# Moving the early steps of a block to its third, fifth and seventh step, doing part of a first step inside a statistics chain, and one scheduling region to the end

## The chip, the cores and the metric

The kernel runs on one core of one Trainium2 chip. The metric is the device time in microseconds of that core, the median of three runs. A profiled execution gives, beside its time, a trace of every instruction on the engines: TensorE (PE, with its weight loads as PEld), VectorE (DVE), ScalarE (ACT), GpSimd (POOL) and SyncE (SP), which here only issues DMAs.

## The reference

The input x is 1 x 384 x 192 x 192 in 32-bit floats. Two residual layers follow each other, each on a group-normalized input (32 groups of 12 channels, over all pixels):

```python
x = x + _L0_conv_ref(_gn(x), ...)
x = x + _L1_conv_ref(_gn(x), ...)
```

The first layer multiplies by a 1152 x 384 matrix (q, k and v), takes the maximum of each 2 x 2 square of pixels, and runs a 3 x 3 depthwise convolution. Of q and k only the norms of their rows and the Gram matrix of 8 heads of 48 channels are needed; four softmaxes, each over the largest 24, 32, 36 or 38 entries of a row, are summed with weights of 0.2 and multiplied by v; a GELU, a doubling of rows and columns, and a 384 x 384 projection give what is added to x. The second layer adds seven depthwise convolutions (13 x 13, and six smaller ones, some dilated), each with its own batch normalization; the kernel merges them into one 13 x 13 filter per channel.

## The kernel before

Channels lie on the 128 partitions, in three chunks (NJ = 3, called j). The kernel goes through four stages.

Statistics. All of x is read once in blocks, chunk after chunk, and each block's mean and variance are taken. When a chunk is complete, its groups' mean and variance are made by `group_stats`, a generator: small matmuls average over the channels of a group, others spread the mean again, VectorE forms the variance's summand, matmuls average that, ScalarE takes the root, VectorE inverts, and last matmuls spread the coefficients to the channels (gn0). Each `yield` is a place where the caller can put other instructions. Since a group is complete with its chunks, the product of the q and k weights with the first pixels can begin early, chunk by chunk: for 18 pairs (B, m) in EARLY (blocks B = 0 to 5, tiles m = 0 to 2 of the q rows, first half of the block) the products with chunks 0 and 1 are made during the statistics (`first_chunk`, `early`, `multiply`, line 420) and put by in the unused space of v (`put_by`, line 431). The last two of these wait for the chain of the third chunk (LATE = 2), and that chain, with nothing to read any more, stands alone at the end of this stage.

First pass. 24 blocks of 8 rows of x; each block has 12 steps, one for each of six tiles m of q and k (m = 0 to 2 is q, 3 to 5 is k) and each half sb of the block. `turns` gives the order of the tiles. A step multiplies (`project`, line 654: six matmuls in the program, each of which the trace shows as two), takes the 2 x 2 maximum on VectorE (`pool`, line 666), adds the bias on ScalarE (line 673), and, after both halves of a tile, `taps` (line 702) adds the eight outer taps of the 3 x 3 filter on VectorE, four in each of two later steps. The products go to one of two PSUM buffers (`qkvps`), so a step can start when the maximum of the step two before it has been read. For a step in EARLY, `fill` (line 260) first copies what was put by back into the PSUM buffer, on ScalarE, and only chunk 2 is multiplied: a short step. When a block's last tile is ready, `turn` (line 731) transposes q and k, and `add_gram` (line 743) adds their product to the Gram matrix; both are done in the fourth to seventh step of the next block. `normalize` (line 634) and GpSimd's `sum_up` (lines 271 to 273) prepare the next block in the seventh step and after.

Second pass and projection. v is made in the same way, the softmaxes run meanwhile, and then 72 projection steps (three chunks of 24 blocks; lines 1418 to 1439) make the first layer's output. In each, ScalarE evicts and stores it (line 1426), and VectorE adds it to loaded sums of x and takes statistics (lines 1434 and 1435). The statistics of the second layer's input are made by `derive`, a generator that calls `group_stats` and that `advance` moves on by one `yield` a projection step. The first two chunks' `derive` run inside the projection; the third one's starts behind it and is moved on once in each block of the convolution.

Convolution. 48 blocks of 8 channels. `arrange` (line 1338) transposes a block's input on VectorE, `patch` (line 1305) corrects its taps, `convolve` (line 1356) makes 8 groups of ten matmuls (as the trace shows them) into one of four PSUM buffers, ScalarE evicts each group into co (line 1364), and `finish` stores it.

The order of instructions on each engine is written out by hand inside a `manual_schedule` region; outside of it, and where one region ends and the next begins, a planner places them. The projection and the convolution were two such regions, with the closing and opening of memory pools between them. Memory that one pool frees is used by the next: the first writer waits for the last reader.

Of the kernel before, what the change touches and what calls it, by code (L numbers as in the profile page):

```python
# [7 lines left out]
F32 = mybir.dt.float32  # L8
# [6 lines left out]
P = 128  # L15
# [24 lines left out]
CC = 8  # L40
# [17 lines left out]
def tile_attn_then_large_kernel_conv(ctx: ExitStack, tc: tile.TileContext, a: dict, out: bass.AP):  # L58
# [42 lines left out]
    def group_stats(pool, psum, mv, name, gw, terms, outs, apart=False):  # L101
# [17 lines left out]
        yield  # L119

# [161 lines left out]
    with (  # L282
# [173 lines left out]
        def early():  # L456
# [5 lines left out]
            for n, (B, m) in enumerate(EARLY):  # L462
# [8 lines left out]
                if n == len(EARLY) - 1:  # L471
                    yield True
# [86 lines left out]
        for _ in range(5):  # L559
            next(last)  # L560
        next(first)
        pc = in_one(last)
        nc.vector.tensor_copy(gn0[:, 2:], pc[:, 2:])
        normalize(0, 0, 2)
        next(first)
        fill(0, 0, 0)
        normalize(0, 1, 2)
        next(first)
# [8 lines left out]
    ctx_l1 = ExitStack()  # L577
    with ctx_v:
# [396 lines left out]
        turns = [m + s * NJ for m in range(NJ) for s in range(2)] + [2 * NJ + m for m in range(NJ)]  # L975
# [427 lines left out]
        with (  # L1403
# [4 lines left out]
            with tc.manual_schedule():  # L1408
                for n in range(NJ * NBB):
                    i, b = divmod(n, NBB)  # L1410
                    if n + 4 < NJ * NBB:
                        load_sum(n + 4)
                    if b == 0 and i > 0:
                        running.append(derive(i - 1, stats1))
                    advance()
                    ps = b2_ps.tile([P, NBK], F32, tag="pj", name="pj")
                    for j in range(NJ):
                        nc.tensor.matmul(  # L1418
                            ps,
                            lhsT=wp[:, j, i * P : (i + 1) * P],  # L1420
                            rhs=v[:, j, b * RB : (b + 1) * RB, :].rearrange("p r w -> p (r w)"),
                            start=(j == 0),
                            stop=(j == NJ - 1),
                        )
                    pj = by.tile([P, 2, RB // 2, WS], F32, tag="pjs", name="pjs", bufs=6)
                    nc.scalar.activation(  # L1426
                        pj.rearrange("p y r w -> p r y w"),
                        ps.rearrange("p (r y w) -> p r y w", y=2, w=WS),
                        AF.Identity,
                        bias=bpj[:, i : i + 1],  # L1430
                    )
                    t = by.tile([P, NBK], F32, tag="cell", name="cell", bufs=1)
                    sm = smj.pop(n)
                    nc.vector.scalar_tensor_tensor(t, sm, quarter[:, i : i + 1], ps, ALU.mult, ALU.add)
                    nc.vector.bn_stats(stats1[:, i, b, :], t)
                    if i == 0:
                        nc.vector.bn_stats(stats_s[:, i, b, :], sm)
                    pd = pds[i]
                    nc.scalar.dma_start(
                        out=bass.AP(  # L1440
                            pd.tensor,
                            pd.offset + b * NBK // 2,
                            [[HS // 2 * WS, P], [P * HS // 2 * WS, 2], [1, NBK // 2]],
                        ),
                        in_=pj.rearrange("p y r w -> p y (r w)"),
                    )
                    if n == NBB + 8:
                        running.append(load_rows(0, nc.gpsimd))
                    if n == NBB:
                        running.append(load_taps(0, nc.gpsimd, 1))  # L1450
                    if n == NBB + 14:
                        running.append(residual(0, nc.vector, 3))
                    if n == NBB + 20:
                        assert not running
                        patch(0)
                        for q in range(3):
                            normalize1(0, q)
                        first = arrange(0, 1)
                    if n > NBB + 20 and n % 3 < 2:
                        next(first, None)  # L1460

                    if n == NBB + 22:
                        running.append(load_rows(1, nc.gpsimd))
                    if n == 2 * NBB + 8:
                        second = residual(1, nc.vector, 3)
                    if n >= 2 * NBB + 8 and (n % 3 == 2 or n > 2 * NBB + 16):
                        next(second, None)
                    if n == 3 * NBB - 4:
                        assert next(first, first) is first and next(second, second) is second
                    if n >= 3 * NBB - 4 and n < 3 * NBB - 1:  # L1470
                        normalize1(1, n - (3 * NBB - 4))
                while running:
                    advance()
                running.append(derive(NJ - 1, stats1))
                advance()

    with (
        tc.tile_pool(name="l2", bufs=1) as l2,  # L1480
        tc.tile_pool(name="more", bufs=1) as more,
        tc.tile_pool(name="lo", bufs=2) as lo,
# [83 lines left out]
```

## Time and profile before

| | us |
|---|---|
| median of 3 runs | 3060.59 |
| lowest and highest | 3058.51, 3060.72 |
| the profiled execution | 3060.02 |
| its span, first to last instruction | 3058.1 |
| TensorE busy | 2932.1 (96%) |
| VectorE busy | 2518.0 (82%) |
| ScalarE busy | 1348.5 (44%) |
| GpSimd busy | 935.2 (31%) |

In the profile a line gives the start, the length, the engine, the line of the kernel, the operation, what it writes from what it reads with shapes, and how many instructions are merged in it. In brackets stands how long the engine was idle before it and what ended the wait. A table by stretch gives, for each engine, the busy time and the number of instructions, then the clock that TensorE was granted as a share of the full one, the DMA share and the bandwidth.

### The profile page before, as it was taken

Reading aid. Unit: us, or ns where it says so; the run is one execution under the profiler, and the core shown is the slowest. Engines: PE = TensorE matmul, PEld = TensorE weight load, DVE = VectorE, ACT = ScalarE, POOL = GpSimd, SP = SyncE. Lnnn points to the kernel's source line nnn. Section 1 sums busy time; section 2 is a strip of 40 time slices with the busy share of each in tenths; the row PEclk is TensorE's granted clock in tenths of the full one; section 3 lists DMA queues with packets and bytes.
Section 4 is the critical chain, followed back from the end, with each engine's and each line's share of the span. In section 5 each row is a group of like instructions: output and inputs, shape, how many; then the busy total and the mean of one; then the engine's idle time right before and its main releaser. Section 6 shows DMA issues by size and latency. Waiting matters only on the chain.

```text
span 3058.1 us, 32274 instructions
## 1 busy us (share of the span) xinstructions
PE 2932.1 (96%) x10860; PEld 1944.7 (64%) x10860; DVE 2518.0 (82%) x3507; ACT 1348.5 (44%) x2465; POOL 935.2 (31%) x1150
## 2 busy tenths in 40 slices
PE   0799999999999999999999999999999999999998
PEld 0355666666666666665555555555777777777776
DVE  6879888787878787879998989888788777777775
ACT  3745554454444444444444444732333333333332
POOL 4242124242423232312222222501333333333332
PEclk9899999999999999999999999999999999999999
DMA  9934243342424242423333332677999999999984
GB/s 392 415 118 146 94 142 126 106 138 97 145 86 153 82 158 77 154 93 101 101 108 125 104 101 70 198 222 203 274 253 243 246 243 243 247 246 243 247 219 116
DMA packets 275926, 525.76 MB, mean 172 GB/s; under 512 B 25954, under 2 KB 190480, under 8 KB 275632
## 3 DMA queue, kind: packets, MB, share of 16 engines
q1 hardware_dynamic: 204432, 326.44, 37.6%
q0 software_dynamic: 49376, 174.29, 18.0%
q10 hardware_dynamic: 21952, 22.95, 2.2%
q8 instruction: 87, 1.43, 0.2%
q14 instruction: 79, 0.65, 0.1%
HBM read 362.23 MB, written 161.37 MB: 171 GB/s over the span
## 4 chain that ended last, share of the span: by engine, by line
PE 85%; DVE 9%; DMA 3%; issue 1%; ACT 1%; POOL 0%; ACTq 0%; POOLq 0%; DVEq 0%
PE qkv L654 46%; PE conv L1356 29%; PE pj L1418 4%; DVE v L702 3%; DMA xs<-in_x 2%; PE av L1110 2%; DVE mx L666 2%; PE gram L743 2%; DVE acc L702 2%; PE tr L731 2%; PE qkv L420 1%; DVE stats L526 1%; DMA smj<-sums 0%; DMA v<-in_x 0%; DVE xp L1338 0%
## 5 line engine op out<-in xcount | busy, mean ns | idle before, releaser
L654 PE MATMUL qkv<-xt,wqk 128*128 128x384 f32 x3312 | 1087.3, 487 | 5.5 <-ACT qkv L260 3.4
L1356 PE MATMUL conv<-xp,wt 128*128 128x288 f32 (+1 forms) x3840 | 917.7, 402 | 2.2 <-ACT co L1364 2.2
L654 PEld LDWEIGHTS qkv<-xt,wqk 128*128 128x128 f32 x3312 | 620.7, 190 | 424.7 <-DVE mx L666 8.0
L1356 PEld LDWEIGHTS conv<-xp,wt 128*128 128x128 f32 x3840 | 729.0, 190 | 188.5 <-ACT co L1364 2.6
L702 DVE SCALAR_TENSOR_TENSOR acc<-pooled,wd,acc 128x384 f32<-128x384 f32 (+2 forms) x1152 | 734.1, 637 | 30.5
L673 ACT ACTIVATE pooled<-mx,bq 128x192 f32<-128x192 f32 x432 | 196.8, 456 | 903.6 <-DVE mx L666 902.2
L1338 DVE STREAM_TRANSPOSE xp<-xn 128x4608 f32<-128x4608 f32 (+1 forms) x107 | 442.0, 4131 | 172.5 <-PE conv L1356 163.4
L666 DVE TENSOR_REDUCE mx<-qkv 128x192 f32<-128x768 f32 x432 | 412.1, 954 | 203.4 <-PE qkv L654 187.5
L654 PE MATMUL qkv<-xt,wv 128*128 128x384 f32 x1728 | 562.4, 487 | 2.5 <-DVE mx L666 2.2
L654 PEld LDWEIGHTS qkv<-xt,wv 128*128 128x128 f32 x1728 | 326.1, 190 | 233.4 <-DVE mx L666 9.8
L1364 ACT ACTIVATE co<-conv,cb 128x288 f32<-128x288 f32 x384 | 191.5, 500 | 600.6 <-PE conv L1356 590.3
L702 DVE SCALAR_TENSOR_TENSOR v<-pooled,wd,v 128x384 f32<-128x384 f32 (+2 forms) x576 | 376.3, 653 | 15.2
L271 POOL TENSOR_TENSOR sum<-xt 128x192 f32<-128x192 f32 x128 | 87.4, 683 | 955.0 <-ACT xt L634 943.1
L1381 POOL DMA_DIRECT2D out<-o x191 | 105.9, 584 | 571.3 <-DVE o L1372 513.6
L634 ACT ACTIVATE xt<-xt,gn 128x768 f32<-128x768 f32 x278 | 275.5, 1014 | 0.0
L1315 POOL TENSOR_TENSOR raw<-raw,up 128x2496 f32<-128x2496 f32 x46 | 230.8, 5017 | 22.5 <-DMA up<-pd 21.3
L1372 DVE STREAM_TRANSPOSE o<-co 128x2304 f32<-128x2304 f32 (+1 forms) x50 | 209.8, 4199 | 19.8 <-ACT co L1364 19.8
L1418 PE MATMUL pj<-v,wp 128*128 128x384 f32 x432 | 144.9, 495 | 0.9 <-ACT gx L1121 0.6
L771 POOL DMA_DIRECT2D zd<-v x96 | 72.0, 757 | 218.9 <-ACT v L762 218.2
L1418 PEld LDWEIGHTS pj<-v,wp 128*128 128x128 f32 x432 | 82.3, 193 | 56.7 <-issue 2.1
L272 POOL TENSOR_TENSOR sum<-sum,xt 128x192 f32<-128x192 f32 x128 | 100.9, 788 | 10.8
L1323 ACT ACTIVATE xn<-raw,par 128x2112 f32<-128x2112 f32 x48 | 102.8, 2142 | 1.2 <-ACT pjs L1426 1.2
(293 smaller groups left out, 1930.1 us busy)
## 6 DMA issues: line engine op xcount, KB each, us to landing
xt<-in_x SPq DMA_DIRECT2D x96, 1152.0 KB, 7.5
wt<-zd SPq DMA_DIRECT2D x46, 1536.0 KB, 13.1
raw<-in_x SPq DMA_DIRECT2D x182, 312.0 KB, 12.1
out<-o POOLq DMA_DIRECT2D x188, 288.0 KB, 5.4
zd<-v POOLq DMA_DIRECT2D x96, 416.0 KB, 4.4
up<-pd SPq DMA_DIRECT2D x184, 156.0 KB, 11.1
xs<-in_x POOLq DMA_DIRECT2D x20, 768.0 KB, 10.2
smj<-sums SPq DMA_DIRECT2D x72, 192.0 KB, 2.7
```

The costliest lines, as they stand in the source:

```text
L634: nc.scalar.activation(xt[:, j], xt[:, j], AF.Identity, bias=gn0[:, j, 1:2], scale=gn0[:, j, 0:1])
L654: nc.tensor.matmul(ps[:, r, : 2 * W], lhsT=wq[:, j, mm * P : (mm + 1) * P], rhs=xt[:, j, r * 2 * W : (r + 1) * 2 * W], start=(j == 0), sto ...
L666: nc.vector.tensor_reduce(mx, ps[:, :, : 2 * W].rearrange("p r (y w x) -> p r w y x", y=2, x=2), AX.XY, ALU.max,)
L673: nc.scalar.activation(pool_t[m][:, k : k + SR, 1 : 1 + WS], mx, AF.Identity, bias=bq[:, m : m + 1])
L702: nc.vector.scalar_tensor_tensor(acc[:, :nt], pool_t[m][:, k0 + dy : k0 + dy + nt, dx : dx + WS], wd[:, m, t : t + 1], acc[:, :nt], ALU.mu ...
L1315: eng.tensor_add(rv, rv, uv.unsqueeze(2).to_broadcast([P, (m1 - m0) * WS, 2]))
L1338: nc.vector.transpose(bass.AP(at.tensor, at.offset, [list(at.ap[0]), [NBQ, n], [1, NBQ], [NQ * NBQ, CC], [ME * NBQ, NE]],), bass.AP(row.te ...
L1356: nc.tensor.matmul(ps[:, t0:t1], lhsT=wt[:, c, o : o + P], rhs=d[:, c, g + 2 * t0 : g + 2 * t1 - 1 : 2, :], start=(g == 1), stop=(g == NGR ...
L1364: nc.scalar.activation(co[:, c], ps, AF.Identity, bias=cb[:, cc : cc + 1])
L1372: nc.vector.transpose(bass.AP(at.tensor, at.offset, [list(at.ap[0]), [2 * W, n], [BC, NBQ], [W, 2], [1, BC]]), bass.AP(of.tensor, of.offse ...
L1381: engines[u % len(engines)].dma_start(out=bass.AP(out.tensor, out.offset + k * CC * HW + (2 * u + t0 * BR) * W, [[ME * UQ * W, CC * NE], [ ...
L1418: nc.tensor.matmul(ps, lhsT=wp[:, j, i * P : (i + 1) * P], rhs=v[:, j, b * RB : (b + 1) * RB, :].rearrange("p r w -> p (r w)"), start=(j = ...
```

## The change

1. `turns` gives the tiles of the first pass in the order 3, 0, 1, 2, 4, 5 instead of 0, 3, 1, 4, 2, 5. The short steps of a block, which were its first, fifth and ninth, are now its third, fifth and seventh.
2. The first step of all is now of tile 3, which is not in EARLY. Two thirds of it, the products with chunks 0 and 1, are made inside the third chunk's chain: those with chunk 0 ahead of the coefficients' matmuls, those with chunk 1 behind them. The last two pairs of EARLY are split into multiply and copy, and stand at other places in that chain: the first multiply ahead of the variance matmuls, the second behind them, and the copies behind the root.
3. `group_stats` has one `yield` more behind the copy of the mean, where `apart` is not set. This is so in the third chunk's chain and in the three calls of `derive`.
4. The `manual_schedule` region of the projection is left open and closed at the very end, so that it holds the convolution too. The loop bodies move to the left and are otherwise the same.

```diff
@@ group_stats
         nc.vector.tensor_copy(mean, ps)
         yield
+        if not apart:
+            yield
@@ early
-                if n == len(EARLY) - 1:
+                if n >= len(EARLY) - LATE:
                     yield True
                 put_by(B, m, ps)
@@ end of the statistics
         last = group_stats(s1, s_ps, mvx, "g0", gw, terms[TWICE[1] + 1 :], (2,))
-        for _ in range(5):
+
+        for _ in range(4):
             next(last)
         next(first)
+        for _ in range(2):
+            next(last)
+        for _ in range(2):
+            next(first)
+        whole = multiply(0, NJ, (0,))
+        next(first)
         pc = in_one(last)
+        multiply(0, NJ, (1,), whole)
+        filled.append(whole)
         nc.vector.tensor_copy(gn0[:, 2:], pc[:, 2:])
-        normalize(0, 0, 2)
-        next(first)
-        fill(0, 0, 0)
-        normalize(0, 1, 2)
-        next(first)
+        for sb in range(2):
+            normalize(0, sb, 2)
@@ first pass
-        turns = [m + s * NJ for m in range(NJ) for s in range(2)] + [2 * NJ + m for m in range(NJ)]
+        turns = [NJ, *range(NJ), *range(NJ + 1, 3 * NJ)]
@@ projection and convolution
-    ctx_l1 = ExitStack()
+    ctx_l1, ctx_p = ExitStack(), ExitStack()
...
-            with tc.manual_schedule():
-                for n in range(NJ * NBB):
+
+            ctx_p.enter_context(tc.manual_schedule())
+            for n in range(NJ * NBB):
...
-        with tc.manual_schedule():
-            patches(l2, 1)
+        patches(l2, 1)
...
+        finish(NK - 1, last, lo, 2, (nc.sync, nc.scalar, nc.gpsimd, nc.sync))
+        ctx_p.close()
     ctx_l1.close()
```

## The prediction

> **What bounds the kernel now.** I read the page first, then a table of busy time by stretch, then the timelines of the four places that the edits touch. In the page: the span, TensorE's busy tenths in 40 slices, the granted clock, and the chain that ended last.
>
> ```profile
> span 3058.1 us, 32274 instructions
> ...
> PE   0799999999999999999999999999999999999998
> ...
> PEclk9899999999999999999999999999999999999999
> ...
> PE 85%; DVE 9%; DMA 3%; issue 1%; ACT 1%; POOL 0%; ACTq 0%; POOLq 0%; DVEq 0%
> ```
>
> TensorE is the bound from the second slice on: an edit is worth the TensorE work or idle time that it takes off the line. Next, busy time of PE, PEld, DVE, ACT and POOL in two blocks of the first pass (12 steps each), the upper with short steps, the lower without:
>
> ```profile
> 295.07:339.92 44.85, 43.52 (x163) 26.44 (x163) 40.70 (x61) 25.44 (x53) 10.17 (x14) 1.00 0.39 131
> ...
> 428.57:479.04 50.47, 50.47 (x187) 31.26 (x186) 42.52 (x63) 24.58 (x53) 17.38 (x25) 1.00 0.40 138
> ```
>
> A full step is 12 matmuls, 3.87 us from start to start; a short one, two thirds of it done early, is 4 matmuls, 1.29 us. Three short steps save 3 x 2.58 = 7.74 us, so block 3 should take 50.47 - 7.74 = 42.73 and takes 44.85. VectorE, busy 40.70, is nearly the bound too. The timeline of that block shows the waits:
>
> ```profile
> 295.07 1.56 PE L654 MATMUL qkv<-xt,wqk 128*128 128x384 f32 x4 [0.87 <-ACT qkv L260]
> ...
> 297.09 8.65 PE L654 MATMUL qkv<-xt,wqk 128*128 128x384 f32 x26 [0.47 <-DVE mx L666]
> ...
> 303.67 2.57 DVE L702 SCALAR_TENSOR_TENSOR acc<-pooled,wd,acc 128x384 f32<-128x384 f32 x4
> ...
> 306.29 0.14 PEld L731 LDWEIGHTS tr<-ident,acc 128*128 128x128 f32 x1 [0.24 <-DVE acc L702]
> ```
>
> The first short step waits for its fill on ScalarE, the step after it for a PSUM buffer behind VectorE's max, and in the fourth step the sixth transpose waits for taps (303.67 to 306.24). From max to max VectorE takes 3.36 to 3.44 us a step, 3.9 and 4.1 in the two steps (tenth, eleventh) beside GpSimd's sums.
>
> **Part 1, the third chunk's chain.** Its timeline:
>
> ```profile
> 161.25 0.35 PE L112 MATMUL g_ps<-g_s,stats 128*32 128x1 f32 x6 [0.75 <-DVE g_s L129]
> ...
> 161.65 2.21 PE L420 MATMUL qkv<-v,wqk 128*128 128x384 f32 x4
> ...
> 163.79 0.58 PE L147 MATMUL g_pc<-g_sb,gmt 32*128 32x2 f32 x2
> ...
> 164.30 2.30 PE L420 MATMUL qkv<-v,wqk 128*128 128x384 f32 x4
> ...
> 164.61 1.03 ACT L483 ACTIVATE xt<-xt,gn 128x768 f32<-128x768 f32 x1
> ```
>
> Both early groups run at half rate for part of their time (850 against 486 ns a matmul): the granted clock is 0.57 from 162 to 166. Now the first group comes ahead of the variance matmuls, the second behind them, then four matmuls of the whole step, the coefficients, and its other four. At full rate: first group 160.36 to 161.76; variance 161.8, 0.55 later than before; root at 162.7; coefficients' input ready at 164.05 (1.1 us of small VectorE instructions, as before). Second group 162.15 to 163.5. The whole step needs the first group's PSUM buffer, whose copy (0.80) now stands behind the root on ScalarE: 163.8 to 165.2. So the coefficients' matmuls, queued behind it, run at 165.2 instead of 163.79, and gn0 and both activations (1.03 each) wait for them: 165.9 and 166.95. The other four matmuls end at 166.75, the first step's last third runs 167.0 to 168.3, and the second step starts at 168.3 instead of 168.02. Its weights landed at 152.4, so no DMA is in the way.
>
> One more short step is worth 2.58, and the start costs 0.3. But block 0 now has short steps in positions 3, 5, 7, one pair after another. I walked it step by step: PE starts when it is free, when the max two steps before is 1.0 us old (297.09 against 296.09), and for a fill 2.2 us after it (3.1 with a normalize in between: 294.23 behind 291.97); VectorE adds its period, 3.85 falling to 2.95 in block 0. Result: the seventh step waits 1.1 for its fill, the eighth 1.1 for its buffer, block 1 starts at 205.3 against 206.12. **-0.8.**
>
> In blocks 1 to 5 the waits at the first two steps vanish: five full steps stand between the seventh and the next block's first, so VectorE catches up. A new wait comes: the third step is short, so the fourth's transposes come early. The sixth needs taps that end 3.44 us after the second step's max; behind it 11 of the fourth step's matmuls queue (3.39), and everything after them. With the second step's start as zero: max at 4.07, taps 7.51, fourth step's end 10.96 instead of 9.69: +1.27. The fills of the fifth and seventh have 1.2 us and more to spare. A block takes 42.73 + 1.27 = 44.0 (block 1 43.6, shorter taps): 219.7 for five against 222.45 traced (206.12 to 428.57). **-2.8.** The same walk over the old order ends 0.4 early at block 7 (478.66 against 479.04), which I take off: part 1 is **-3.2**. Bounds: 0 if VectorE falls behind everywhere, -9.5 if the transposes wait nothing (3.2 + 5 x 1.27), which the row at 306.29 speaks against. Order of the nine tiles, fills and copies moved on ScalarE: same counts, hidden under it (25 of 44 us busy).
>
> A rule weighed: the Trainium skill's page "TensorE: Matmul & The Clock Gate" (What's actually happening) says a window of 3413 ns in which TensorE idles halves its clock for the next. Here TensorE was busy 2.44 us of the window 159.0 to 162.4, and the half rate came nevertheless; but only 0.77 us of that were wide matmuls, the rest one-column ones. Windows with 1.85 us of wide ones kept the rate, with 0.92 (2077.3 to 2080.7) lost it. The changed chain has about 1.7 in it. By the page's words full rate in both; by the rows it lies between, nearer 1.85. I take full rate; half rate costs 1.3 (part 1 is then -1.9).
>
> **Part 2, the extra step of the statistics generator.** In the projection the second chunk's mean holds TensorE:
>
> ```profile
> 2079.64 0.61 DVE L1434 SCALAR_TENSOR_TENSOR cell<-smj,quarter,pj 128x384 f32<-128x384 f32 x1 [1.54 <-DMA smj<-sums]
> ...
> 2081.66 1.01 PE L123 MATMUL g_pb<-g_mean,gmt 32*128 32x1 f32 x4 [3.45 <-DVE g_mean L118]
> ...
> 2082.60 6.57 PE L1418 MATMUL pj<-v,wp 128*128 128x384 f32 x12
> ```
>
> The mean's copy is queued on VectorE behind a step that waits for a load, TensorE idles 3.45, and the next six matmuls take 4.00 instead of 1.93 (clock 0.55 from 2083 to 2088). With one step more, a projection step (1.93) runs before the wait, from 2078.05; its buffer is free since 2077.6. Then the mean's matmuls at 2081.66, the next step at 2082.2, and the one after at 2084.15, where before it started at 2089.31: -5.16, less 0.2 for variance matmuls that come a step later. VectorE allows it: from 2082.2 to 2116 it idled 4.8. First chunk: -0.2 (0.64 of weight-load wait at 2028.8). Third chunk: inside the convolution, no wait on TensorE. Part 2 is **-5.0**. Bounds: -0.5, if the load and store traffic that causes the stall holds the following steps too; -5.5.
>
> **Part 3, one region.** At the seam between projection and convolution:
>
> ```profile
> 2124.54 9.70 PE L1356 MATMUL conv<-xp,wt 128*128 128x288 f32 x40
> ...
> 2126.51 8.27 DVE L1338 STREAM_TRANSPOSE xp<-xn 128x4608 f32<-128x4608 f32 x1
> ...
> 2135.02 0.80 DVE L1184 BATCH_NORM_AGGREGATE mvs<-stats_s 128x2 f32<-128x144 f32 x1
> 2135.91 1.68 ACT L1364 ACTIVATE co<-conv,cb 128x288 f32<-128x288 f32 x4 [10.26 <-DVE mvs L1184]
> ...
> 2136.46 45.58 PE L1356 MATMUL conv<-xp,wt 128*128 128x288 f32 x190 [2.21 <-ACT co L1364]
> ```
>
> The first eviction waits for the last reader of stats_s, and that was put behind the 8.27 us transpose; four PSUM buffers fill, TensorE idles 2.21. In one region the order is as written: the aggregate comes before the transposes, done by about 2128, and the 2.21 go: **-2.2**. The transposes come 2.5 later, done at 2137.9, and what is late next is the patch of block 1's taps. A rule speaks against it: "GPSIMD Engine Reference" (Specifications) says GpSimd contends with VectorE instructions of two SBUF inputs, and the patch is one, falling into GpSimd's add of 4.92 at 2136.57. The row: a 0.16 us instruction there took 4.35. Waiting out the add, the patch ends at 2143.1, as it did before (2143.06); block 1 now starts at 2143.6. By rule and row no cost; 1.5 if it slips.
>
> **Sum.** -3.2 - 5.0 - 2.2 = -10.4. The profiled execution took 3060.02 around its span of 3058.1, so 3049.6; it lies 0.57 under the median, so 3050.2.
>
> **Rivals.**
> - Half rate stays: 1.3 in the chain and 2.1 in the projection (six matmuls at 0.32 more) come back: -7.0, 3053.6. For it: the windows don't start with the kernel. Chance 0.17.
> - The projection's stall is the DMAs': at 2081.57 ScalarE too waited 4.68 for a store. Then TensorE waits one step later and part 2 is -0.5: -5.9, 3054.7. Against: loads and stores land within 3 us again from 2083. Chance 0.13.
> - Part 1 doesn't do what it says, the short steps' gain stays in VectorE's queue: -7.2, 3053.4. Chance 0.07.
> - Slower: GpSimd's sums fall beside the short steps, and VectorE takes 3.9 instead of 3.4 us in eight steps of a block: 4.4 behind, less 1.2 of slack, 3.2 a block, +16 in five, -10.4: 3066. It decides against the change from 2.1 us a block on (3.75 a step). Against: the sums follow the normalizes of steps 7 to 10, and stay at steps 10 and 11. Chance 0.05.
>
> **Numbers.** The first case has 0.58. 0.2%, 6.1 us, is what a measurement can tell: 3054.5 divides. Above it lie the slower case, most of the DMA case and parts of the middle two: faster 0.80, same 0.15, slower 0.05. The range takes in the first three cases and both sides of their bounds: 3046.5 to 3055.8.
>
> **What would show it.** Second step at 168.3, block 1 near 205, blocks of 44.0 with the only wait in the fourth step; no 3.45 wait for the mean and no half clock near 2080; the convolution's first 80 matmuls in one piece. Wrong if blocks 2 to 5 exceed 44.85, or the projection still stalls 4 us in its third chunk.

## The result and the profile after

The changed kernel takes 3053.05 us (median of ten runs, 3050.53 to 3056.25), the kernel before beside it 3060.40 (3056.56 to 3063.55): a ratio of 0.9978, with a 95% interval of 0.9970 to 0.9986. That is 7.35 us less, between 4.3 and 9.2. I had said 3050.2, between 3046.5 and 3055.8, so the time lies in the range, 2.85 above the point, and 1.45 below the 3054.5 that I had set as the line between faster and the same; the interval of the difference reaches over that line. The profiled execution of the changed kernel took 3051.11.

The page of the changed kernel, first the span, the two rows of slices, the chain that ended last, then the convolution's row of the groups (busy time, mean length, and after the bar the idle time before it):

```profile
span 3049.3 us, 32277 instructions
...
PE   0799999999999999999999999999999999999998
...
PEclk9899999999999999999999999999999999999999
...
PE 87%; DVE 7%; DMA 4%; issue 1%; ACT 1%; POOL 0%; ACTq 0%; DVEq 0%; POOLq 0%
...
L1364 PE MATMUL conv<-xp,wt 128*128 128x288 f32 (+1 forms) x3840 | 917.5, 402 | 0.0
```

The span is 8.8 shorter, VectorE's share of the chain went from 9% to 7%, and the convolution's matmuls wait for nothing any more (2.2 before). The lines of the kernel are shifted: 654, 666, 702 and 731 became 662, 674, 710 and 739, the projection's 1418 and 1434 became 1427 and 1443, and the convolution's 1356 and 1364 became 1364 and 1372.

**The blocks.** Busy time by stretch of block 3 and of block 6, with the same columns as before (length; PE, PEld, DVE, ACT, POOL; clock, DMA share, bandwidth):

```profile
294.00:338.01 44.01, 42.98 (x163) 26.61 (x162) 40.47 (x61) 25.42 (x52) 10.16 (x13) 1.00 0.40 133
426.04:476.51 50.47, 50.47 (x187) 31.26 (x186) 41.42 (x61) 23.43 (x49) 16.06 (x23) 1.00 0.36 128
```

Block 3 takes 44.01 instead of 44.85. The timeline of its fourth step shows what is left of waiting:

```profile
302.81 2.57 DVE L710 SCALAR_TENSOR_TENSOR acc<-pooled,wd,acc 128x384 f32<-128x384 f32 x4
...
303.70 0.71 PE L739 MATMUL tr<-ident,acc 128*128 128x128 f32 x5
...
305.44 0.33 PE L739 MATMUL tr<-ident,acc 128*128 128x128 f32 x1 [1.03 <-DVE acc L710]
...
305.61 4.04 PE L662 MATMUL qkv<-xt,wqk 128*128 128x384 f32 x12
```

Five transposes run, the sixth stands until VectorE's taps of 302.81 are done at 305.38, and the step's matmuls stand behind it. It is the only wait of TensorE's matmuls in the block.

**The third chunk's chain.** Its timeline:

```profile
160.81 1.56 PE L422 MATMUL qkv<-v,wqk 128*128 128x384 f32 x4
...
162.30 0.35 PE L112 MATMUL g_ps<-g_s,stats 128*32 128x1 f32 x6
...
162.71 1.56 PE L422 MATMUL qkv<-v,wqk 128*128 128x384 f32 x4
...
164.11 1.56 PE L422 MATMUL qkv<-xt,wqk 128*128 128x384 f32 x4
...
165.59 0.38 PE L149 MATMUL g_pc<-g_sb,gmt 32*128 32x2 f32 x2
...
167.30 5.09 PE L662 MATMUL qkv<-xt,wqk 128*128 128x384 f32 x15
```

All early groups take 1.56 for four matmuls, which is the full rate; before it was 2.21 and 2.30.

**The projection.** Its timeline around the small matmuls of the first two calls:

```profile
2035.48 1.28 ACT L90 ACT_TABLE_LOAD   x1 [2.47 <-DMA pd<-pjs]
...
2036.88 0.56 ACT L1435 ACTIVATE pjs<-pj,bpj 128x384 f32<-128x384 f32 x1
...
2037.47 0.61 DVE L1443 SCALAR_TENSOR_TENSOR cell<-smj,quarter,pj 128x384 f32<-128x384 f32 x1 [2.29 <-DMA smj<-sums]
...
2039.74 0.38 PE L149 MATMUL g_pc<-g_sb,gmt 32*128 32x2 f32 x2 [1.20 <-DVE g_sb L143]
...
2079.87 0.60 PE L125 MATMUL g_pb<-g_mean,gmt 32*128 32x1 f32 x4 [1.25 <-DVE g_mean L118]
...
2080.40 4.14 PE L1427 MATMUL pj<-v,wp 128*128 128x384 f32 x12
...
2091.78 0.60 PE L149 MATMUL g_pc<-g_sb,gmt 32*128 32x2 f32 x4 [1.03 <-DVE g_sb L143]
```

The mean's wait fell from 3.45 to 1.25, and the twelve matmuls behind it take 4.14 instead of 6.57. But the coefficients' matmuls, which had waited 0.3 at most, now wait 1.20 in the first call and 1.03 in the second. In the first call VectorE's part of the root, the inversion, stands behind the addition of 2037.47, which waited 2.29. The row names the loaded sums, but these had landed at 2034.81; the addition starts when ScalarE's eviction of the same step ends, at 2037.44. That eviction stands behind the root on ScalarE, which came late: ScalarE had stood 2.47 in front of a store and then loaded a table for the root (ACT_TABLE_LOAD) for 1.28.

**The seam.** The timeline of the start of the convolution:

```profile
2118.69 21.63 PE L1364 MATMUL conv<-xp,wt 128*128 128x288 f32 x90
...
2120.95 0.79 DVE L1192 BATCH_NORM_AGGREGATE mvs<-stats_s 128x2 f32<-128x144 f32 x1
...
2121.82 0.50 ACT L1372 ACTIVATE co<-conv,cb 128x288 f32<-128x288 f32 x1 [2.03 <-DVE mvs L1192]
...
2123.14 9.20 DVE L1346 STREAM_TRANSPOSE xp<-xn 128x384 f32<-128x384 f32 x2
```

The aggregate stands ahead of the transposes, the first eviction follows it at 2121.82, and the 90 matmuls up to the end of this view run in one piece.

So the two profiled spans differ by 2.9 in part 1 (from the mean's first matmul in the chain, 158.51 and 158.90, to block 7, 479.04 and 476.51), 0.2 between block 7 and the projection, 3.15 in the projection (152.49 and 149.34 from its first matmul to the convolution's), 2.5 in the convolution's first 80 matmuls and 0.5 behind its last. The statistics ended 0.4 later. The order of the three parts is not the one that I had predicted: -3.2, -5.0, -2.2.

### The profile page after: what moved, and what is told of

Read it like the earlier page. It is cut to its first block, busy times and chain, and to the rows that moved or that the text cites. A ratio compares the mean times of both kernels' runs of the same rounds, so it can differ in the third digit from the quotient of the medians.

```text
span 3049.3 us, 32277 instructions
## 1 busy us (share of the span) xinstructions
PE 2925.8 (96%) x10860; PEld 1943.1 (64%) x10860; DVE 2513.4 (82%) x3507; ACT 1348.1 (44%) x2465; POOL 935.7 (31%) x1150
## 4 chain that ended last, share of the span: by engine, by line
PE 87%; DVE 7%; DMA 4%; issue 1%; ACT 1%; POOL 0%; ACTq 0%; DVEq 0%; POOLq 0%
PE qkv L662 48%; PE conv L1364 29%; DVE v L710 3%; PE pj L1427 3%; DMA xs<-in_x 2%; PE av L1118 2%; PE gram L751 2%; PE tr L739 2%; DVE mx L674 1%; PE qkv L422 1%; DVE acc L710 1%; DMA smj<-sums 1%; DVE stats L528 1%; DMA pd<-pjs 0%; DMA v<-in_x 0%
```

## The experiments

Each stretch of time below is read from one trace. In all of them the first chunk of the projection took 46.54 or 46.55 us and the convolution from its 81st matmul 900.90, so that all differences lie in the stretches told of.

### Each part alone

Part 1 alone, on the kernel before (with the new lines of the chain, which are those of the change):

```diff
-        turns = [m + s * NJ for m in range(NJ) for s in range(2)] + [2 * NJ + m for m in range(NJ)]
+        turns = [NJ, *range(NJ), *range(NJ + 1, 3 * NJ)]
@@ group_stats, behind the copy of the mean
+        if name == "g0":
+            yield
```

> The kernel before with part 1 alone: the new order of tiles, the first step inside the third chunk's chain, and the extra step of the generator only in that chain. Measured from the first matmul of the third chunk's mean to the first matmul of block 7: before 320.53 us (158.51 to 479.04), the changed kernel 317.61 (158.90 to 476.51). Theory, each part works on its own stage alone: 317.6 again, blocks 2 to 5 of 44.0 each, fourth step with a wait of 1.27 in its transposes, projection stage still 152.5 us with a wait of some 3.4 for the second chunk's mean; some 2.9 us less in all, 3057.5, ratio 0.9990. Rival, the clock of the chain depends on where the free-running windows fall: the eight early matmuls of the chain at 850 instead of 390 ns of pitch somewhere, 318.9. Rival, part 1 is worth nothing by itself: 320 or more.

Measured: 317.62 from the chain to block 7; time 3057.27 against 3059.85, ratio 0.9991 (0.9983 to 1.0000). The stretch is that of the whole change to a hundredth. The 2.9 of part 1 depend on no other part.

Part 2 alone, on the kernel before:

```diff
@@ group_stats, behind the copy of the mean
+        if name[:2] == "g1":
+            yield
```

> The kernel before with part 2 alone, the extra step of the statistics generator in its three later calls. Measured from the projection's first matmul to the convolution's first: before 152.48 us, changed kernel 149.34, where I had predicted 147.3. Theory: the mean's wait of 3.45 falls to 1.3 to 1.7 and no window is at half clock, but the coefficients' matmuls, one projection step behind the root, wait 1.0 to 1.2 in each of the first two chunks, since VectorE's part of the root is queued behind an addition that waits for its loaded sums; 149.3 again, 3.1 less in all, 3057.3. Rival, those new waits were chance of the loads in one execution: 147.3, 5.2 less, 3055.2. Rival, the loads hold every step: the wait for the mean only becomes a wait of another step, 152. The chain of the third statistics chunk should show the half clock again near 162 to 166 if the small matmuls before it are its cause, and not always if the windows decide by chance.

Measured: 3059.78 against 3059.85, ratio 1.0000 (0.9992 to 1.0008). The projection took 150.54. The part that I held for the largest is worth nothing that a time shows. The timeline of this kernel's projection:

```profile
2042.82 0.38 PE L149 MATMUL g_pc<-g_sb,gmt 32*128 32x2 f32 x2 [1.38 <-DVE g_sb L143]
...
2083.02 0.60 PE L125 MATMUL g_pb<-g_mean,gmt 32*128 32x1 f32 x4 [1.35 <-DVE g_mean L118]
2083.55 5.83 PE L1420 MATMUL pj<-v,wp 128*128 128x384 f32 x12
```

The mean's wait is short, as predicted. But the coefficients of the first call wait 1.38, as in the changed kernel (here too ScalarE stood in front of a store, 2.65, loaded the table, and the addition ahead of the inversion began when its eviction ended), and the matmuls behind the mean run at half rate all the same. The clock column (the last but two) of three pairs of stretches in that execution, each pair one window of the clock, 3.41 us, and the next, cut a little short:

```profile
2131.60:2134.90 3.30, 1.10 (x5) 0.60 (x4) 3.20 (x7) 0.77 (x2) 0.00 (x0) 1.00 1.08 238
2135.00:2138.30 3.30, 3.30 (x8) 2.36 (x7) 3.27 (x2) 0.81 (x3) 3.01 (x1) 0.50 1.07 370
2080.40:2083.70 3.30, 1.95 (x9) 1.06 (x9) 1.93 (x4) 0.53 (x1) 0.00 (x0) 1.00 1.06 319
2083.80:2087.10 3.30, 3.30 (x6) 1.74 (x6) 3.16 (x8) 0.58 (x1) 0.00 (x0) 0.50 0.99 325
158.70:162.00 3.30, 2.33 (x27) 2.02 (x25) 1.00 (x6) 1.42 (x3) 2.69 (x6) 1.00 0.10 35
162.10:165.40 3.30, 3.30 (x7) 1.63 (x7) 1.10 (x8) 1.56 (x3) 0.92 (x2) 0.50 0.09 30
```

A window in which TensorE was busy 1.10, 1.95, or 2.33 us of the 3.30 shown (the last with the small matmuls of the chain) is followed by one at half clock, in the chain, in the projection, and here at the seam too, where the kernel of the first profile had none.

Part 3 alone, on the kernel before:

```diff
-            with tc.manual_schedule():
+            ctx_p.enter_context(tc.manual_schedule())
...
-        with tc.manual_schedule():
...
+        ctx_p.close()
```

> The kernel before with part 3 alone, one region from the projection to the end. Measured from the convolution's first matmul to its 81st: before 21.56 us, changed kernel 19.08. Theory, the eviction's wait for the aggregate that stood behind the long transpose was all that held it: 19.1, no wait of a matmul for co, everything else as before, projection 152.5; 2.5 less, 3057.9. Rival, the rest of the convolution gives some of it back (block 1's taps or the later evictions are late): the convolution of 922.5 us ends up less than 2 us shorter.

Measured: 19.08 for the convolution's first 80 matmuls, nothing given back later; time 3056.36 against 3059.85, ratio 0.9990 (0.9982 to 0.9998). That is 3.5, more than the 2.5 of the trace. With the runs below, the seam of the old order took 21.56, 21.54 and 21.55 in three traces, and 23.24 and 23.25 in two, in which the idle 2.2 was followed by a window at half clock. So part 3 takes away 2.5 in some executions and 4.2 in others.

The chain of this kernel is that of the kernel before, instruction for instruction, and shows no half rate (1.56 for each group, against 2.21 and 2.30):

```profile
162.53 1.56 PE L420 MATMUL qkv<-v,wqk 128*128 128x384 f32 x4
...
164.77 1.56 PE L420 MATMUL qkv<-v,wqk 128*128 128x384 f32 x4
```

### The kernel before, once more

> The kernel before, unchanged, for one more trace. In the one that I predicted from, the projection took 152.49 us, with a wait of 3.45 for the second chunk's mean and two windows at half clock; the two experiments that leave this part as it was took 150.46 and 150.76, with waits of 2.58 and 2.57 and one such window. Theory, the traced execution was a slow draw: 150 to 151 again, and the chain's half clock near 162 to 166 may be there or not. Rival, 152.5 is the kernel before, and the other two executions owe their 150.6 to the other parts of the change: 152.5 again.

Measured: 150.72, with the mean's wait at 2.82 and one window at half clock; 3058.87, ratio 1.0001 (0.9991 to 1.0010).

```profile
2082.27 0.60 PE L123 MATMUL g_pb<-g_mean,gmt 32*128 32x1 f32 x4 [2.82 <-DVE g_mean L118]
2082.80 5.83 PE L1418 MATMUL pj<-v,wp 128*128 128x384 f32 x12
```

So in the execution from which I predicted, this stage took long: 152.49, where the three others without the extra step took 150.46, 150.76 and 150.72. The mean's wait follows the sums: the addition ahead of the mean's copy waited 1.54, 0.68, 0.66 and 0.91 for them in these four traces, and TensorE 3.45, 2.58, 2.57 and 2.82, which is 1.90 to 1.91 more each time.

### What the projection gives back

One more step ahead of the coefficients' matmuls, in the changed kernel:

```diff
@@ group_stats, ahead of pc = psum.tile(...)
+        if name[:2] == "g1":
+            yield
```

> The changed kernel with one more step of the generator ahead of the coefficients' matmuls, in the three later calls alone. Theory, these matmuls come too early for VectorE's part of the root: their waits of 1.20 and 1.03 vanish and nothing takes their place, projection stage 147.1 instead of 149.34, time 3050.8 instead of 3053.05. Rival, the loads and stores are what limits here, and TensorE waits one step later for a buffer instead: 149.3, 3053.

Measured: projection 148.35, time 3050.29 (ratio to the kernel before 0.9970, 0.9958 to 0.9981).

```profile
2041.56 0.38 PE L151 MATMUL g_pc<-g_sb,gmt 32*128 32x2 f32 x2
...
2080.65 0.60 PE L125 MATMUL g_pb<-g_mean,gmt 32*128 32x1 f32 x4 [2.17 <-DVE g_mean L118]
...
2093.41 0.60 PE L151 MATMUL g_pc<-g_sb,gmt 32*128 32x2 f32 x4
```

Both waits of the coefficients are gone. The mean's wait was 2.17 in this execution (an addition of VectorE waited 2.21 for its sums, against 1.28), which is 0.9 of the 1.2 by which my 147.1 was missed.

Two more steps, the second ahead of the mean's matmuls as well:

```diff
@@ group_stats, behind the extra step of the change
+        if name[:2] == "g1":
+            yield
@@ group_stats, ahead of pc = psum.tile(...)
+        if name[:2] == "g1":
+            yield
```

> The changed kernel with two steps more in the three later calls of the generator, one ahead of the mean's matmuls and one ahead of the coefficients'. Theory, with both, no small matmul comes before VectorE is ready: the mean's wait (2.17 with one step more, 1.25 in the changed kernel) falls to 0.3 or less, projection 146.5 instead of 148.35, time 3048.5. Rival, the loads and stores behind VectorE's and ScalarE's lateness hold the next projection step's buffer instead: 148.3 and 3050.3 as with one.

Measured: projection 147.98, time 3050.51 (0.9970, 0.9958 to 0.9981). The mean waits no more, but the variance's matmuls behind it wait 0.75, and another small matmul 0.96 at 2101.45. The rival's number is right: against one step more nothing is gained in the time, and 0.4 in the trace. What waits is a small matmul, though, and not a projection step's buffer.

The extra step of the change left out of the first of the three calls:

```diff
-        if not apart:
+        if not apart and name != "g1_0":
```

> The changed kernel without the extra step in the first of the three later calls of the generator. Five traces with the extra step in all three calls took 50.1 to 52.5 us for the projection's second chunk, where that first call runs, and 52.0 to 53.7 for the third; five without it took 48.9 to 49.2 and 53.0 to 57.0. Theory, the second chunk gives back what the third one gains: without the step there, 48.9 in the second and 52.0 to 53.7 in the third, projection 147.5 to 149.2, time 1.2 to 2.5 less than the changed kernel, 3051. Rival, the two are coupled by the loads (a quicker second chunk moves the rows' loads against the third chunk's statistics): third chunk at 54 or more, 3053.

Measured: 48.91 and 53.07 for the second and third chunk, projection 148.53, time 3050.78 (0.9971, 0.9960 to 0.9982). The medians of this kernel and the changed one lie 2.3 apart, as expected, though the intervals of their ratios overlap. Its second chunk (48.91) lies below all five traces with the extra step in that call (50.09 to 52.49).

```profile
2032.27 1.28 ACT L90 ACT_TABLE_LOAD   x1 [0.43 <-ACT pjs L1435]
...
2037.31 0.38 PE L149 MATMUL g_pc<-g_sb,gmt 32*128 32x2 f32 x2
...
2080.10 0.60 PE L125 MATMUL g_pb<-g_mean,gmt 32*128 32x1 f32 x4 [1.99 <-DVE g_mean L118]
```

This is the plainest of the three: taken out of the one call where it stands beside the load of the first rows, the extra step costs nothing, and its gain in the next call stays. It also shows what the step did there: without it ScalarE loads the root's table at 2032.27, ahead of the store, and the store's wait (2.63, at 2036.86) comes behind the root; with it the root comes behind the store.

The sums loaded further ahead, on the kernel before, with no extra step anywhere:

```diff
-                    if n + 4 < NJ * NBB:
-                        load_sum(n + 4)
+                    if n + 6 < NJ * NBB:
+                        load_sum(n + 6)
@@ ahead of the projection
-                for n in range(4):
+                for n in range(6):
                     load_sum(n)
@@ load_sum
-            smj[n] = b2.tile([P, NBK], F32, tag="smj", name=f"smj_{n}", bufs=5)
+            smj[n] = b2.tile([P, NBK], F32, tag="smj", name=f"smj_{n}", bufs=7)
```

> The kernel before with one size changed: the sums of x are loaded six projection steps ahead instead of four (seven buffers instead of five). Theory, the second chunk's mean is late because VectorE's queue stands behind additions that wait for these loads while the rows of block 1 are loaded: VectorE's waits of 1.5 to 2 near the 37th and 55th projection step vanish, the mean's wait (2.6 to 3.5 in three executions with this generator) falls by as much, to about 1, and the third chunk's clock stays whole: projection 149 instead of 150.5 to 152.5, time 1.5 to 3 less. Rival, the stores hold ScalarE and so TensorE's buffers whatever VectorE does: 150.5, 3059.8.

Measured: no addition near the mean waits for its sums; the mean's wait is 1.99, no window of the projection is at half clock; projection 148.40; time 3057.52, ratio 0.9995 (0.9986 to 1.0003).

```profile
2080.99 0.60 PE L123 MATMUL g_pb<-g_mean,gmt 32*128 32x1 f32 x4 [1.99 <-DVE g_mean L118]
2081.52 4.14 PE L1418 MATMUL pj<-v,wp 128*128 128x384 f32 x12
...
2082.95 0.61 DVE L1434 SCALAR_TENSOR_TENSOR cell<-smj,quarter,pj 128x384 f32<-128x384 f32 x1 [2.02 <-ACT pjs L1426]
```

The loads are part of the cause: without their lateness the same order of instructions is 2.1 to 4.1 quicker here. They are not all of it, since 1.99 and not 1 is left of the wait. What is left is VectorE's own queue: from 2074.20 to the mean's copy at 2080.78 it has four additions with their statistics and three transposes, and no idle time above 0.09. (The row at 2082.95 comes behind the mean: there VectorE waits for ScalarE, which stood 4.65 in front of a store.) That agrees with the 1.9 by which the mean's wait exceeds the addition's in the four traces above. In the time the gain can't be told from none; the profiled execution had its window at half clock at the seam (23.25), which hides 1.7 in its span.

### The fourth step's wait in the blocks

The transposes one step later, in the changed kernel:

```diff
-                            at(s + 4 + i, turn_next, b, i)
-                            at(s + 5 + i, gram_next)
+                            at(s + 5 + i, turn_next, b, i)
+                            at(s + 6 + i, gram_next)
@@ begin
-                acc = a1.tile([P, R + 1, WS], F32, name=f"acc_{b}_{m}", tag="acc", bufs=8)
+                acc = a1.tile([P, R + 1, WS], F32, name=f"acc_{b}_{m}", tag="acc", bufs=9)
```

(Left out: the six pooled tiles of q and k become one tile, to make room, and `begin_attention` moves by the same step.)

> The changed kernel with the transposes of a block one step later (in the next block's fifth to eighth step instead of its fourth to seventh), which needs a ninth acc buffer; the six pooled tiles of q and k become one tile to make room. Theory, the 1.27 us that each of blocks 1 to 5 waits in its fourth step is the wait for taps: it vanishes there. My step-by-step walk with that wait taken out and the transposes moved gives 43.3 for block 1 and 43.6 for blocks 2 to 5 instead of 43.6 and 44.0, because VectorE, with short steps at 3, 5, 7 close together, then holds the fill of the seventh step; 1.8 us less, 3051.2. If the taps alone are to blame and VectorE has room, 42.75 a block, 6 us less. Rival, the wait is not the taps but VectorE's own time: 44.0 a block, 3053.

Measured: 44.2 a block, time 3054.62 (ratio to the kernel before 0.9985, 0.9978 to 0.9991). The table of block 3 and its timeline:

```profile
295.10:339.30 44.20, 43.48 (x163) 26.37 (x162) 40.32 (x61) 25.42 (x52) 10.30 (x14) 1.00 0.40 133
```

```profile
308.59 0.91 PE L663 MATMUL qkv<-xt,wqk 128*128 128x384 f32 x2 [0.40 <-ACT qkv L262]
...
310.00 1.68 PE L663 MATMUL qkv<-xt,wqk 128*128 128x384 f32 x4
...
312.00 0.92 PE L752 MATMUL gram<-qk,qk 128*96 128x96 f32 x8 [0.32 <-ACT qk L742]
```

The transposes' wait is gone, and the fifth step waits for its fill instead; behind it the next step waits for a PSUM buffer, and the Gram matmuls for ScalarE's copy of the transposed q and k. The fill and the buffer both wait for VectorE's max. So with short steps at 3, 5, 7 and this order VectorE is the next to hold the block; neither 43.6 nor 42.75 came, and the rival's 44.0 lies nearest. Besides, the last block of the pass ended 1.6 later, as its transposes are the last work of that stage (1494.43 from block 7 to the projection, 1492.84 in the changed kernel).

The same with the short steps at 5, 7 and 9:

```diff
-        turns = [NJ, *range(NJ), *range(NJ + 1, 3 * NJ)]
+        turns = [NJ, NJ + 1, *range(NJ), *range(NJ + 2, 3 * NJ)]
```

> As the run before it, and the short steps at the fifth, seventh and ninth step (order of tiles 3, 4, 0, 1, 2, 5). Theory: the transposes wait for nothing, and five full steps of the block before plus four of this one let VectorE catch up before the first short step: 42.75 a block (three times 2.58 less than 50.47), block 0 0.9 longer than in the changed kernel; by the walk block 7 starts 5.0 us earlier than in the changed kernel, 3048.0. Rival, VectorE, with GpSimd's sums beside the steps after the seventh, holds the last short step: 43.7 a block, 3052.

Measured: block 7 starts 312.73 behind the chain's mean, 4.9 earlier than in the changed kernel; time 3048.65 (0.9966, 0.9954 to 0.9979).

```profile
293.67:336.47 42.80, 42.80 (x164) 26.61 (x163) 40.61 (x61) 25.31 (x52) 10.21 (x14) 1.00 0.41 138
```

The stretch is one block long and begins 1.26 behind the block's first matmul at 292.41; from first matmul to first matmul blocks 2 to 5 take 42.76 each, block 1 43.10. TensorE is busy all the time; nothing is left of waits. VectorE still has 40.6 of the 42.8.

And those positions with the transposes where they were:

> The changed kernel with the short steps at the fifth, seventh and ninth step (order of tiles 3, 4, 0, 1, 2, 5), the transposes where they were. With the transposes one step later as well a block took 42.8 us; with them later and the short steps left at 3, 5, 7 it took 44.2. Theory, the place of the short steps decides: with four full steps ahead of the first short one, the transposes of the fourth step come after their taps in any case, and my walk gives 43.7 a block, because the fourth to sixth step are then longer and bunch the short ones behind them; 0.4 less at block 7 than the changed kernel, 3052.6. Rival, the taps' wait was all: 42.8 a block, 4.9 less, 3048.

Measured: 43.64 in each of blocks 1 to 4 and 43.73 in block 5, as the walk said; block 7 0.7 earlier than in the changed kernel; time 3052.79 (0.9982, 0.9973 to 0.9990). The timeline of block 3 has one wait of TensorE:

```profile
324.63 15.75 PE L662 MATMUL qkv<-xt,wqk 128*128 128x384 f32 x48 [0.64 <-ACT qkv L262]
```

It is the last short step's, for its fill. So neither edit alone removes the waits, and both together do.

### All of it

The changed kernel with the last positions, the later transposes in all blocks but the last, the two steps more, and the sums six steps ahead:

```diff
+                        late_by = 4 if b == NB - 1 else 5
-                            at(s + 4 + i, turn_next, b, i)
-                            at(s + 5 + i, gram_next)
+                            at(s + late_by + i, turn_next, b, i)
+                            at(s + late_by + 1 + i, gram_next)
```

> The changed kernel with short steps at 5, 7, 9, the transposes one step later in all blocks but the last of the first pass, two more steps of the generator in its three later calls, and the sums loaded six steps ahead. Theory, the gains add up: block 7 at 312.7 us behind the start of the mean (changed kernel 317.6), from there to the projection 1492.9 as in the changed kernel, because only the last block's late transposes made that 1494.4, projection 146.5 to 148, the convolution as in the changed kernel: a span of 3042 to 3043, time 3044.5. Rival, the stretch from block 7 to the projection stays at 1494.4, and the projection at 148 to 150 because the loads take what the order gives: 3047 to 3048.5.

Measured: 312.74 to block 7, 1492.84 from there, projection 147.20, seam 19.08; time 3044.40 against 3058.02, ratio 0.9955 (0.9942 to 0.9967), 13.6 us less than the kernel before. Its span is 7.0 below the changed kernel's:

```profile
span 3042.3 us, 32277 instructions
```

The stretch to block 7 is that of the later and wider order (312.73), and the one behind it that of the changed kernel, so that the 1.6 came from the last block's transposes alone. The projection is 0.8 below that with two steps more (147.98): the sums loaded ahead, worth 2.1 to 4.1 on the kernel before, add little where the steps have already taken the waits away. That is one trace each.

## Why the prediction was right, and where it was not

The stages over all traces, those with the old form of a part against those with the new one:

| stretch | old | new | difference of means |
|---|---|---|---|
| chain's mean to block 7 | 320.53, 320.83, 320.15, 320.14, 320.09 | 317.61, 317.62, 317.62, 317.61, 317.61 | -2.7 |
| block 7 to the projection | 1492.97 to 1493.06 | 1492.84 to 1492.86 | -0.2 |
| projection, second chunk | 48.92, 48.92, 49.23, 48.92 | 50.09, 50.28, 52.32, 50.88, 52.49 | +2.2 |
| projection, third chunk | 57.03, 55.00, 54.98, 55.26 | 52.71, 53.73, 52.50, 52.49, 52.04 | -2.9 |
| convolution's first 80 matmuls | 21.56, 21.54, 23.24, 23.25, 21.55 | 19.08 in all | -3.15 |

The traces are those in which the part has exactly the one form or the other: runs with further steps of the generator or with the sums ahead are left out of the projection's rows, and runs with another order of the blocks out of the first two. The sum of the last column is -6.75, against -7.35 measured (4.3 to 9.2). What the 0.2 behind block 7 comes from stays open.

**Part 1: right, in its steps too.** Predicted -3.2, found -2.9 in the two profiles and -2.7 over all: 2.4 of it in blocks 1 to 5, where I had 2.8, and 0.3 up to block 1, where I had 0.8. Three of the five old executions reach block 1 as early as the new ones (47.11, 47.25 and 47.26 behind the mean, against 47.14 and 47.15): the short step that block 0 gains, 2.58, is used up by its own waits and by the start. Blocks 2 to 5 take 44.0, as said, with the one wait where it was said (block 1 takes 43.95 instead of 43.6); the second step of all starts at 168.68, which is 168.3 as predicted with the 0.4 by which this execution's statistics ended later; the seventh and eighth step of block 0 wait 0.76 and 1.09 for fill and buffer (1.1 each predicted). Block 1 starts at 206.04 instead of 205.3; 0.4 of that is the later start, 0.35 the walk's error in block 0. My lower bound of -9.5, however, was wrong in its reason: with the transposes' wait taken out and the short steps left where they are, the block stays at 44.2. The next wait behind it is VectorE's.

**The clock in the chain.** The half rate of the old chain was there in two of five executions (the first profile and the run of part 2 alone), and in none of the nine traces with the new chain. I called the half rate a property of the old order; it is a matter of where the window falls. The Trainium skill says the same in "TensorE: Matmul & The Clock Gate" (What's actually happening): the window runs freely and does not start with the kernel. My guess that wide matmuls (384 or 288 columns) count and small ones don't fits all 14 traces. Count the windows of 3.41 us from 140 us to 3030, placed in each trace by the edges of its half-rate windows. Eleven at full rate were followed by one at half: each held at most 1.54 us of matmuls other than the small ones of the statistics. Every window that kept the rate held at least 1.56. The total busy time does not divide them: 2.45 lost the rate, 1.74 kept it. The idle window of the rule that I weighed is not needed; here the measurement decides. In the new chain, with wide matmuls on either side of the small ones, no position of a window holds less than 1.56, in the old one it can be 0.34; so by this count the new order has no bad position, and in nine executions it showed none. (The ends of matmuls in a trace are modelled, so the border is near 1.55 and no sharper.) The half rate is also cheap: the two executions with it took 320.53 and 320.83, the other three 320.09 to 320.15, so it costs 0.4 to 0.7 at block 7, where I had 1.3 as its price. At the second step of all it is no more than 0.5 to 0.65 already (9.51 and 9.65 behind the mean, against 8.99 and 9.00), because at full rate the coefficients wait 0.40 for VectorE and the first step 0.52 for its fill (trace of part 3 alone).

**Part 2: wrong in size.** Predicted -5.0, found -0.7 (+2.2 - 2.9), and 0.0 +- 2.4 as a time. Two terms failed.

The first is "First chunk: -0.2". The extra step moves the whole rest of the first call one projection step later. There the root on ScalarE falls behind a store that waits 2.5 to 3.3 us, while the first block's rows are loaded (four loads of 312 KB and four of 156 each, by the page's list of DMA issues and the timeline), and the inversion on VectorE behind an addition that waits 1.9 to 2.4 for ScalarE's next eviction. (I had put that down to the sums, in the expectation of part 2 alone too; in all five traces they landed 2.6 us or more before the addition began.) The coefficients' matmuls then wait 1.20, 1.38, 1.73, 1.99 and 1.95 in five traces, and in two of these a window at half clock follows. I looked for the wait that goes and for the steps right behind it, but not for the next small matmul of the same chain. The run without the step in this call shows it: there the root is ahead of the store, and its second chunk is back at 48.91.

The second is the -5.16 of the second chunk's call. In the pair of profiles it is right to 0.03: the third chunk's fifth step starts 1.53 earlier than it did (2074.58 against 2076.11), the ninth 6.67 earlier (2084.68 against 2091.35), so 5.14 lie between them. Of this 0.8 is lost again before the chunk ends (57.03 to 52.71), for the most part in the new wait of 1.03. And the profile of before was an execution with a wait of 3.45 and two windows at half clock; in three more traces of that code the wait was 2.58, 2.57 and 2.82 with one window, and the third chunk took 55.0 to 55.3, not 57.0. I took one execution's stall for the kernel's. The bound of -0.5 "if the load and store traffic that causes the stall holds the following steps too", and the rival made of it (-5.9, 3054.7), came nearer in the number. Its reason is borne out only in part: the traffic is there at the new wait of the first call, but it does not hold the third chunk's steps. One step more ahead of the coefficients, or none in the first call, and the gain is there with the same traffic.

**Part 3: right in mechanism, too small.** Predicted -2.2; the wait itself was 2.21, the trace gives 2.5, and the mean over traces 3.15, because in two of five executions the idle 2.2 is followed by a window at half clock, 1.7 more. The patch of block 1's taps beside GpSimd's addition cost nothing, as said.

So the sum missed by 3.65: 4.3 too much in part 2 and 0.5 in part 1, against 1.0 too little in part 3 and 0.2 behind block 7. That the time lies within the range is owed to its width, since its upper end took in part 2's bound of -0.5; that it lies 2.85 from the point, and not the 4.8 of the first two errors, is in part luck, as errors of both signs met. Two more rivals lie nearer to 3053.05 than the point does, and for other reasons than theirs. With part 1 worth nothing it would be 3053.4, but the blocks are 44.0. With the half rate kept it would be 3053.6, and that is half true: in the chain it is gone, but in the projection one window at half rate came in three of the five traces with the step in all three calls. The slower rival did not come: VectorE's busy time in block 3 is 40.47, against 40.70 before.

## What to carry to other kernels

A step that waits in one trace should be priced from several executions, when loads or the clock stand behind the wait; here three further traces cut the price of the same stall by 2 us. When a chain of small dependent instructions is moved by one step, every later link of it moves too, and each has to be looked at where it now falls, in every place that calls it. An idle stretch of TensorE of 1.35 to 3.45 us can be worth more than its length, because in a part of the executions a window of 3.4 us at half rate follows it; in these traces it did so when 1.54 us or less of wide matmuls were left in one window. And where a wait is put down to one of several, look at when the others ended: an addition that seemed to wait for a load began when ScalarE's eviction ended.

## What was not expected

Half clock does not need an idle window: TensorE was busy 1.95 of 3.30 us (a step at 2080.4 to 2083.7), and 2.33 with small matmuls, and still lost half of the next window. The same instructions kept the full rate in other executions. And the seam's wait of 2.2, the same in all five executions, costs 2.5 or 4.2, with nothing between: where the wait and the small stretches beside it fell into one window, this held 1.20 or 1.21 us of matmuls and the next was at half rate; where they fell across two, each held 1.90 or more and the rate stayed.
